# A convolution, attention and expert kernel: small operands moved to PSUM, row sums reordered, one norm partly on GpSimd

## The chip, the core and the metric

The kernel runs on one core of a Trainium2 chip, as one launch. The core has five engines, each with a queue of its own that is worked through in order: TensorE (PE in the profile, PEld where it loads weights), VectorE (DVE), ScalarE (ACT), GpSimd (POOL) and SyncE (SP, which here only issues transfers). The metric is the device time of the launch in microseconds. A ratio is the new time over the old one, so below 1 is faster.

## The reference, cut to what matters

Four images of 256 channels and 32 by 32 places (1024 tokens each) go through one layer:

```python
x = x + L0_conv_ref(_ln_c(x), ...)     # norm over channels, then the mixer below
t = _to_tokens(x)
t = t + L0_ffn_ref(_ln_t(t), ...)      # experts: 2 of 8 for each token

# the mixer, per image (names cut)
xn  = layernorm(xs); xc = xn in 4 groups of 64 channels
xm  = selective scan of each group (128 inner channels, 16 states) + skip * xc
R   = gated, depthwise and pointwise convolutions of xm
xm2 = convolutions of [xs, R]
x_local  = depthwise convolution of xm2
x_global = softmax attention of xm2, 8 heads of 32 channels
x_out = gelu(layernorm([x_local, x_global] @ fc.T))
out   = projection of layernorm(3x3 depthwise of ln_hw(x_out))

# the experts
top_w, top_i = top_k(xf @ Wg, 2); top_w = softmax(top_w)
out += w[:, e] * (gelu(xf @ W1[e] + b1[e]) @ W2[e] + b2[e])   # for each expert e
```

All data are float32. The softmax of a token's two gate values is computed as 1 / (1 + exp(m2 - m1)) and its complement.

## The kernel before, in words

**Order of the work.** The order on every engine is the order of the program text: a manual schedule fixes it. The program is made of Python generators that issue a few instructions and then `yield` a number of beats. A loop of beats (`beat`, `start`, `drain`) resumes each generator when its time has come, one after the other. So a generator that yields one beat more comes one beat later against all the others, on all engines, and the queues of the engines never change their order at run time.

**The scan.** Each image has eight parts (four groups, two halves of 512 tokens), and each part 16 steps; one step is one beat. A step works on a tile of 128 partitions (32 channels by 4 states) by 512 tokens: ACT makes the decay (L718, three steps ahead), DVE the inflow (`dBu`, L728) and the scan (L739), POOL multiplies by the output coefficients (L747), PE sums over the states (L757).

**Beside the scan.** While image b is scanned, other generators work on images before and after it. With part 3 of image b ends a first half; then come `attention(b - 1)` and the work joined to it (`joined`), `local(b - 1)`, the 3x3 convolution of image b - 2 (`around`) and the norm of the image b + 1 (`normalised`). Until 30 of attention's 32 steps are issued no step of the scan is issued; then `resume` starts part 4 and the rest runs beside it. For b = 1 this is the first attention, and `normalised(2)`, the third image's norm, starts in the same beat as it. The attention of the fourth image comes after all scans, between tiles of the experts.

**The norm of an image** (`normalised`, L524 on): after the loads, PE averages two chunks of 128 channels with a matrix of constants (`column_mean`, accumulating over the chunks), DVE subtracts the mean, POOL squares, PE averages the squares, ACT makes two roots (r1, r2). Then for each chunk POOL multiplies by r1 (L556), DVE by r2 (L558), SP stores the first product, POOL scales the second (L561), and for the third image `own_taps` adds one ACT and two DVE operations (L572, L579) and a store.

**Attention** (L1112 on): a step is one of two groups of four heads, one half of the queries and one block of 128 keys. PE makes the logits of the next step (`st`, L1126), ACT their exponentials (`e`, L1136), PE multiplies this step's by the values (`av<-e,v`, L1175). DVE adds the exponentials of an even and an odd block (L1183), and `sum_pair` (L1144) has PE sum the rows of the pair with a matrix of ones (`av<-e,every`, L1147). A pair is put on a list at the end of an odd step. It is summed at the head of the next odd step, or, in the last five steps, at the head of the next step whatever its parity, in both cases before the next logits are issued.

**Routing** (`dispatch`, L1797 on): with the norm's r (L1858) the gate values are scaled, `first_largest` finds the largest and the second largest of the eight (m_1, m_2) and their experts, one expert bit per token goes through two matmuls (`places`, L1886, L1887) to be counted, `ex` and `w_1` become the two weights (L1881, L1891, L1903 to L1911), and XR, the token's row with its number, weights and expert, is scattered by POOL to rows sorted by expert. `gp` and `cp` are banks in PSUM of which these steps cut pieces (`w1()`, `w3()`); m_1, m_2, r, mr, ex and w_1 are [128, 8, 1] tiles in SBUF. For the first two images (`beside`) the normalised rows are made by ACT from r and mr, for the others by DVE. Routing of image 0 runs beside the scan of image 2, that of image 1 beside the scan of image 3, the others between expert tiles.

**The tables.** `series` (L2133) and `table` (L2019) turn the counts into a list of tiles: which expert, and where its rows start. All of it is done by DVE on [128, 8] or [128, 8, 8] tiles. The table of the first series is made in the last part of the scan, at 1411 to 1420 us; those after it between expert tiles.

PSUM has eight tiles of one bank each, tag `ps`, from which each user takes the next free one. `a2` (16 tiles of 512) and `a4` (8 of 1024) are pools of SBUF tiles.

Of the kernel before, what the change touches and what calls it, by code (L numbers as in the profile page):

```python
# [78 lines left out]
def network(  # L79
# [71 lines left out]
    with tc.tile_pool(name="w_conv", bufs=1) as wp, tc.tile_pool(  # L151
# [251 lines left out]
        def a2(name, rows=P):  # L403
            return act2.tile([rows, HALF], F32, tag="a2", name=name)
# [118 lines left out]
        def normalised(b):  # L523


            place_xn(b)
            xn = XN[b]

            def part(c, h):
                return xn[:, c, ds(LEFT + h * HALF, HALF)]  # L530

            yield 4

            def centre(h, mean):
                for c in range(NC2):
                    nc.vector.tensor_tensor(part(c, h), part(c, h), mean, ALU.subtract)

            yield from in_turn(
                range(2), lambda h: column_mean(f"mean_{b}_{h}", [part(c, h) for c in range(NC2)]),
                centre,  # L540
            )
            r1, r2 = a4(f"r1_{b}"), a4(f"r2_{b}")
            for h in range(2):
                sq = [a2(f"sq_{b}_{h}_{c}") for c in range(NC2)]
                for c in range(NC2):
                    nc.gpsimd.tensor_tensor(sq[c], part(c, h), part(c, h), ALU.mult)
                yield 1
                var = column_mean(f"var_{b}_{h}", sq)
                yield 2
                root(r1[:, half(h)], var, eps6)  # L550
                yield 1
                root(r2[:, half(h)], var, eps11, scale=1.0 + 1e-5)
                yield 1
            for c in range(NC2):
                xl = a4(f"xl_{b}_{c}")
                nc.gpsimd.tensor_tensor(xl, xn[:, c, LEFT:], r1, ALU.mult)  # L556
                yield 2
                nc.vector.tensor_tensor(xn[:, c, LEFT:], xn[:, c, LEFT:], r2, ALU.mult)  # L558
                yield 1
                nc.sync.dma_start(XL[b][:, c, :], xl)  # L560
                nc.gpsimd.tensor_scalar(  # L561
                    xn[:, c, LEFT:], xn[:, c, LEFT:], col("norm_w", c), col("norm_b", c),
                    ALU.mult, ALU.add,
                )
                yield 1
                if b in XD and b < B - 1:
                    yield from own_taps(b, c, xl)
# [539 lines left out]
        def attention(b):  # L1107
# [32 lines left out]
            log_exp()  # L1140
            ahead = logits(*steps[0])
            pairs, accs, ending = [], [None, None], []

            def sum_pair():  # L1144
                kt, acc, es = pairs.pop()
# [18 lines left out]

            for at, (g, h, kt) in enumerate(steps):
                es = ahead
                if pairs and (kt % 2 or at > len(steps) - 6):
                    sum_pair()
                if at + 1 < len(steps):
                    ahead = logits(*steps[at + 1])  # L1170
                if kt == 0:

                    accs = [ps(f"av_{b}_{g}_{h}_{w}") for w in range(2)]
                for i in range(4):
                    nc.tensor.matmul(  # L1175
                        accs[0][ts(i, HD)], v8[:, kt, ts(4 * g + i, HD)], es[i],
                        start=(kt == 0), stop=(kt == NK - 1),
                    )
                if kt % 2 == 0:
                    first = es  # L1180
                else:
                    for i in range(4):
                        nc.vector.tensor_tensor(first[i], first[i], es[i], ALU.add)  # L1183
                    pairs.append((kt, accs[1], first))
                    if ending:
                        end_block(*ending.pop())
                if kt == NK - 1:
                    ending.append((g, h, *accs))
                if at == len(steps) - 3:
                    T["attended", b] = True  # L1190
                yield 1
# [204 lines left out]
        def tiles():  # L1396
# [28 lines left out]
            def table(n):  # L1425
                tables_of.add(n)
                s, i = order[n]
                if s < rest and i == 0:
                    tables[s] = experts.series(s, temp)

            def load(n):
                s, i = order[n]
# [206 lines left out]
class Experts:  # L1639
# [158 lines left out]
    def dispatch(self, b, X1, XR, root, log_exp, recent):  # L1798
# [67 lines left out]
        )  # L1866
        beside = b < self.B - 2
        if beside:
            mr = s1("mr")
            nc.vector.scalar_tensor_tensor(mr, mv[:, :, 0:1], -1.0, r, ALU.mult, ALU.mult)  # L1870
        m_1, oh1, at1 = self.first_largest(lg, "1", w1, eq)
        yield 1
        lg2 = lg
# [3 lines left out]

        oh = s3("oh")
        nc.vector.tensor_tensor(oh, oh1, oh2, ALU.add)
        ex, w_1 = s1("ex"), s1("w_1")  # L1880
        nc.vector.tensor_tensor(ex, m_2, m_1, ALU.subtract)  # L1881
        yield 4 if beside else 1
        cp = bank(f"places_{b}")
        flat = oh.rearrange("p t e -> p (t e)")
        W = NT * NE
        nc.tensor.matmul(cp[:, 0:W], self.before, flat, start=True, stop=True)  # L1886
        nc.tensor.matmul(cp[:, W : 2 * W], self.every, flat, start=True, stop=True)  # L1887

# [12 lines left out]
            if t % (4 if beside else 2) == 1:  # L1901
                yield 1
        nc.vector.tensor_scalar(w_1, ex, 1.0, None, ALU.add)  # L1903
        nc.vector.reciprocal(w_1, w_1)
        nc.gpsimd.iota(
            XR[:, :, C : C + 1], [[P, NT], [0, 1]], base=b * N, channel_multiplier=1,
            allow_small_or_imprecise_dtypes=True,
        )
        nc.vector.tensor_copy(XR[:, :, C + 1 : C + 2], w_1)
        nc.vector.tensor_tensor(ex, ex, w_1, ALU.mult)  # L1910
        nc.vector.tensor_tensor(XR[:, :, C + 2 : C + 3], ex, w_1, ALU.subtract)  # L1911
        nc.vector.tensor_scalar(XR[:, :, C + 3 : C + 4], at2, float(NE), None, ALU.add)
        yield 1

# [101 lines left out]
        nc.vector.tensor_reduce(ntile.rearrange("p a e -> p e a"), steps, AX.X, ALU.add)  # L2016
        return ntile

    def table(self, temp, keep, name, n, ntile, which, done=None, kinds=NE):  # L2019


        nc = self.nc
        ends = keep(f"ends_{name}", [P, 1, kinds])
        nc.vector.tensor_tensor_scan(
            ends[:, 0, :], self.every[:, 0:kinds], ntile[:, 0, :], 0.0, ALU.mult, ALU.add
        )
        starts = temp(f"starts_{name}", [P, 1, kinds])
        nc.vector.tensor_tensor(starts, ends, ntile, ALU.subtract)
        S = [P, n, kinds]
        past = temp(f"past_{name}", S)  # L2030
        nc.vector.tensor_tensor(past, which, ends.to_broadcast(S), ALU.is_ge)
        inside = temp(f"inside_{name}", S)
        nc.vector.tensor_tensor(inside, which, starts.to_broadcast(S), ALU.is_ge)
        nc.vector.tensor_tensor(inside, inside, past, ALU.subtract)
        expert = keep(f"expert_{name}", [P, n, 1])
        nc.vector.tensor_reduce(expert, past, AX.X, ALU.add)
        nc.vector.tensor_scalar(expert, expert, float(kinds - 1), None, ALU.min)
        if kinds > NE:
            second = temp(f"second_{name}", [P, n, 1])
            nc.vector.tensor_scalar(  # L2040
                second, expert, float(NE), float(-NE), ALU.is_ge, ALU.mult
            )
            nc.vector.tensor_tensor(expert, expert, second, ALU.add)

        nc.vector.tensor_tensor(which, which, starts.to_broadcast(S), ALU.subtract)
        if done is not None:
# [12 lines left out]
        table = self.m0.tile([P, 2, n], mybir.dt.int32, name=f"table_{name}")  # L2059
        nc.vector.tensor_copy(table[:, 0, :], expert.rearrange("p n a -> p (n a)"))  # L2060
        nc.vector.tensor_scalar(
            table[:, 1, :], first.rearrange("p n a -> p (n a)"), float(self.SPARE), None, ALU.add
        )
        return (expert, table), starts, ends
# [65 lines left out]
        nc.vector.tensor_copy(self.missed, self.sum_of(temp, "missed", missed))  # L2130
        return table

    def series(self, s, temp):  # L2133

        if s == self.WIDE:
            return self.wide_series(temp)
# [30 lines left out]
        if s:  # L2167
            nc.vector.tensor_tensor(ntile, ntile, self.done, ALU.subtract)
        table, starts, ends = self.table(
            temp, self.kept, s, n, ntile, which, self.done if s else None  # L2170
        )
        taken = temp(f"taken_{s}", [P, 1, NE])
        nc.vector.tensor_scalar(taken, starts, -1.0, float(n), ALU.mult, ALU.add)
# [346 lines left out]
```

## Time and profile before

| what | value |
|---|---|
| median of three runs | 2169.73 us (2165.35 to 2173.6) |
| profiled execution | 2167.03 us, its span 2165.3 us |
| PE busy | 1931.0 us, 89% of the span |
| DVE busy | 1540.5 us, 71% |
| ACT busy | 1212.3 us, 56% |
| POOL busy | 1043.4 us, 48% |
| mean granted clock of TensorE | 0.961 |

Shares over the whole span mix stages with different limits. The span goes, roughly, like this: preparation to 60 us; scans of the first images to 430; the first attention, 430 to 531; scans to 790; the second attention, 790 to 888; scans to 1190; the third attention, to 1290; the last scans to 1439; convolutions of the fourth image and expert tiles to 1592; the fourth attention to 1681; expert tiles, with the last image's end between them, to 2165. A row of the profile in order of time gives start and length in us, engine, line of the kernel, operation, what is written from what, shapes, and in brackets how long the engine had been idle and what released it. Buffer numbers are left out of the names, and rows that follow each other with the same line are merged (x4).

### The profile page before, as it was taken

How to read it: one execution, taken by the hardware profiler on the slowest of the kernel's cores; microseconds unless marked ns; L12 is line 12 of the kernel's file. 1: busy time of each engine (PE TensorE's matmuls, PEld its weight loads, DVE VectorE, ACT ScalarE, POOL GpSimd, SP SyncE). 2: the span in 40 equal slices, each digit the busy share in tenths (PEclk: the TensorE clock that was granted, in tenths of full speed). 3: DMA queues.
4: the chain of work that ended last, by engine and by line, in shares of the span. 5: the costliest groups of instructions: out<-in, count | busy, mean ns of one | idle time of the engine just before them, and what ended most of it. 6: DMA issues, size and time to landing. Idle time of an engine off the chain costs nothing. (4 is left out here: it accounts for less than half of the span.)

```text
span 2165.3 us, 28187 instructions
## 1 busy us (share of the span) xinstructions
PE 1931.0 (89%) x8690; PEld 867.6 (40%) x8690; DVE 1540.5 (71%) x2252; ACT 1212.3 (56%) x2272; POOL 1043.4 (48%) x931
## 2 busy tenths in 40 slices
PE   6778778999977999988779999669999989999996
PEld 2113112322211332223123223216652668888885
DVE  4989999957998989698899888987265354321121
ACT  4665657668777677776466876615268423222221
POOL 0887887812787850476877016662021012522131
PEclk8888999999999999998999999989999999999998
DMA  3555544401444431153634203444230165777764
GB/s 105 148 157 130 124 118 103 101 28 57 103 116 117 104 75 40 25 141 92 176 87 105 83 6 94 109 164 135 84 99 23 47 198 161 242 229 188 213 184 131
DMA packets 157087, 251.40 MB, mean 116 GB/s; under 512 B 34740, under 2 KB 101332, under 8 KB 156664
## 3 DMA queue, kind: packets, MB, share of 16 engines
q1 hardware_dynamic: 136560, 223.47, 37.3%
q0 software_dynamic: 12720, 17.32, 4.1%
q10 hardware_dynamic: 7640, 8.65, 1.2%
q8 instruction: 72, 1.18, 0.2%
q14 instruction: 95, 0.78, 0.1%
HBM read 137.22 MB, written 36.62 MB: 80 GB/s over the span
## 5 line engine op out<-in xcount | busy, mean ns | idle before, releaser
L747 POOL TENSOR_TENSOR dA<-hs,cs 128x512 f32<-128x512 f32 x512 | 681.1, 1339 | 376.9 <-DVE hs L739 249.8
L718 ACT ACTIVATE dA<-dts,A 128x512 f32<-128x512 f32 x512 | 359.0, 718 | 161.4 <-DMA dts<-dt 76.9
L757 PE MATMUL yp<-dA,quads 128*32 128x512 f32 x1024 | 286.3, 640 | 89.3 <-POOL dA L747 76.6
L2350 POOL DMA_INDIRECT Y<-ys,dest x68 | 109.6, 1612 | 424.3 <-DVE ys L2343 417.3
L1136 ACT ACTIVATE e<-st 128x512 f32<-128x512 f32 x512 | 263.7, 606 | 89.4 <-PE st L1126 89.2
L2337 ACT ACTIVATE hs<-h,b 128x256 f32<-128x256 f32 (+1 forms) x256 | 110.6, 478 | 343.6 <-PE h L2332 256.7
L728 DVE TENSOR_TENSOR dBu<-dts,bs 128x512 f32<-128x512 f32 x384 | 259.6, 677 | 46.0 <-PE bs L710 10.8
L739 DVE TENSOR_TENSOR_SCAN hs<-dA,last,dBu 128x512 f32<-128x512 f32 x192 | 243.6, 1269 | 3.0 <-issue 2.1
L2365 PE MATMUL y<-w,hs 128*128 128x256 f32 (+1 forms) x1088 | 242.4, 382 | 0.0
L2332 PE MATMUL h<-xT,w 128*128 128x256 f32 (+1 forms) x1024 | 239.7, 390 | 0.8 <-DVE xT L2295 0.8
L739 DVE TENSOR_TENSOR_SCAN hs<-dA,dBu 128x512 f32<-128x512 f32 x192 | 231.6, 1206 | 0.7 <-PE var L438 0.7
L1183 DVE TENSOR_TENSOR e<-e,e 128x512 f32<-128x512 f32 x256 | 168.2, 718 | 77.8 <-ACT e L1136 47.8
L2332 PEld LDWEIGHTS h<-xT,w 128*128 128x128 f32 x1024 | 195.2, 192 | 41.7 <-issue 8.0
L2365 PEld LDWEIGHTS y<-w,hs 128*128 128x128 f32 (+1 forms) x1088 | 197.3, 188 | 36.1 <-issue 9.0
L2295 DVE COPY xT<-xp 128x512 f32<-128x512 f32 (+1 forms) x36 | 23.3, 646 | 249.4 <-PE xp L2291 249.1
L710 PE MATMUL bs<-u,xpwT_s 128*32 128x512 f32 x1024 | 162.9, 669 | 40.3 <-DVE hs L739 17.3
L1126 PE MATMUL st<-qk 32*128 32x512 f32 x1024 | 174.0, 638 | 0.3
L757 PEld LDWEIGHTS yp<-dA,quads 128*32 128x32 f32 x1024 | 51.3, 114 | 303.4 <-POOL dA L747 198.7
L1175 PE MATMUL av<-e,v 128*32 128x512 f32 x1024 | 139.5, 604 | 0.0
L1953 POOL DMA_INDIRECT XS<-XR,to x64 | 65.4, 1022 | 92.0 <-ACT e L1136 53.9
L1126 PEld LDWEIGHTS st<-qk 32*128 32x128 f32 x1024 | 59.5, 183 | 115.3 <-issue 85.6
L1147 PE MATMUL av<-e,every 128*32 128x512 f32 x512 | 85.2, 596 | 2.7 <-DVE e L1183 2.6
(357 smaller groups left out, 2640.5 us busy)
## 6 DMA issues: line engine op xcount, KB each, us to landing
dts<-dt SPq DMA_DIRECT2D x512, 128.0 KB
w<-in_W_dram SPq DMA_DIRECT2D x124, 512.0 KB
cs<-cd SPq DMA_DIRECT2D x512, 64.0 KB
xs<-XS SPq DMA_DIRECT2D x32, 260.0 KB
xd<-xn SPq DMA_DIRECT2D x64, 128.0 KB
xn<-in_x_dram SPq DMA_DIRECT2D x8, 512.0 KB
XL<-xl SPq DMA_DIRECT2D x8, 512.0 KB
xl<-XL SPq DMA_DIRECT2D x4, 1024.0 KB
```

The source lines that it names most:

```text
L710: nc.tensor.matmul(bs[r], xpwT_s[:, n, s : s + 1].to_broadcast([P, 32]), T[b, n, "u"][:, half(h)], start=True, stop=True,)
L718: nc.scalar.activation(dA, T[b, n, h, "dts", g][:, 0, :], AF.Exp, scale=A[:, g, n, q : q + 1])
L728: nc.vector.tensor_tensor(dBu, T[b, n, h, "dts", g][:, 1, :], T[b, n, h, "bs", q], ALU.mult)
L739: nc.vector.tensor_tensor_scan(hs, T[b, n, h, "dA", i], dBu, 0.0 if h == 0 else last, ALU.mult, ALU.add)
L747: nc.gpsimd.tensor_tensor(dA, hs, T[b, n, h, "cs", q], ALU.mult)
L757: nc.tensor.matmul(T[b, n, h, "yp"][ts(g, 32)], quads, T[b, n, h, "dA", q * GD + g], start=False, stop=(q == GS - 1),)
L1126: nc.tensor.matmul(sts[i], k[r, ts(kt, P)], q[r, half(h)], start=True, stop=not shifted)
L1136: ins = nc.scalar.activation(es[i], sts[i], AF.Exp, scale=1.0 / HD**0.5)
L1175: nc.tensor.matmul(accs[0][ts(i, HD)], v8[:, kt, ts(4 * g + i, HD)], es[i], start=(kt == 0), stop=(kt == NK - 1),)
L1183: nc.vector.tensor_tensor(first[i], first[i], es[i], ALU.add)
L2332: nc.tensor.matmul(hp[:, i, :], w1(c, k0 + i), xT[:, c, :], start=(c == 0), stop=(c == NC2 - 1))
L2365: nc.tensor.matmul(yp[ts(k % parts, n), ts(t % 2, C)], hidden(k)[:, ds(t * P, n)], w2(k), start=(k < parts), stop=(k >= NHC - parts),)
```

## The change

Three parts of the program are edited.

1. Routing: the tiles ex and w_1 become pieces of the bank `places`, which is now claimed before the yield that stood between them and the matmuls. m_1 is copied to a piece of the gate's bank before it is subtracted; for the first two images ACT copies r to such a piece, and mr is made from the copy. The reciprocal is written to its column of XR at once, and the copy to that column (L1909) goes. The first table gets a bank of its own in PSUM: the counts are copied to it, and ends, starts and inside are pieces of it.
2. Attention: the rule that a pair is summed at the head of a step, before the logits, holds for the third image only. For the others a pair is summed in the next step, behind its product with the values.
3. Norm of the third image: POOL adds the two chunks, and later the two squares, so that `column_mean` gets one chunk instead of two. The sums and squares lie in halves of r1 and r2 and no longer in four `a2` tiles. The generator yields two beats more before the means and one more before each half's second step.

```diff
@@ normalised
+            r1, r2 = a4(f"r1_{b}"), a4(f"r2_{b}")
+            one_chunk = b == 2
+            if one_chunk:
+                for h in range(2):
+                    nc.gpsimd.tensor_tensor(r1[:, half(h)], part(0, h), part(1, h), ALU.add)
+                yield 2
             yield from in_turn(
-                range(2), lambda h: column_mean(f"mean_{b}_{h}", [part(c, h) for c in range(NC2)]),
+                range(2), lambda h: column_mean(
+                    f"mean_{b}_{h}",
+                    [r1[:, half(h)]] if one_chunk else [part(c, h) for c in range(NC2)],
+                ),
                 centre,
             )
-            r1, r2 = a4(f"r1_{b}"), a4(f"r2_{b}")
             for h in range(2):
-                sq = [a2(f"sq_{b}_{h}_{c}") for c in range(NC2)]
+                if one_chunk:
+                    sq = [v[:, half(h)] for v in (r1, r2)]
+                else:
+                    sq = [a2(f"sq_{b}_{h}_{c}") for c in range(NC2)]
                 for c in range(NC2):
                     nc.gpsimd.tensor_tensor(sq[c], part(c, h), part(c, h), ALU.mult)
+                if one_chunk:
+                    nc.gpsimd.tensor_tensor(sq[0], sq[0], sq.pop(), ALU.add)
+                    yield 1
                 yield 1
@@ attention
+            late = b == B - 2
...
-                if pairs and (kt % 2 or at > len(steps) - 6):
+                if late and pairs and (kt % 2 or at > len(steps) - 6):
                     sum_pair()
...
+                if pairs and not late:
+                    sum_pair()
                 if kt % 2 == 0:
                     first = es
@@ tiles
-                    tables[s] = experts.series(s, temp)
+                    tables[s] = experts.series(s, temp, None if s else ps("first_table"))
@@ dispatch
         if beside:
-            mr = s1("mr")
-            nc.vector.scalar_tensor_tensor(mr, mv[:, :, 0:1], -1.0, r, ALU.mult, ALU.mult)
+            mr, r_too = s1("mr"), w1()
+            nc.scalar.copy(r_too, r)
+            nc.vector.scalar_tensor_tensor(mr, mv[:, :, 0:1], -1.0, r_too, ALU.mult, ALU.mult)
...
-        ex, w_1 = s1("ex"), s1("w_1")
-        nc.vector.tensor_tensor(ex, m_2, m_1, ALU.subtract)
+        cp = bank(f"places_{b}")
+        W = NT * NE
+        ex, w_1 = (
+            cp[:, ds(7 * W + k * NT, NT)].rearrange("p (t a) -> p t a", a=1) for k in range(2)
+        )
+        first = w1()
+        nc.vector.tensor_copy(first, m_1)
+        nc.vector.tensor_tensor(ex, m_2, first, ALU.subtract)
         yield 4 if beside else 1
-        cp = bank(f"places_{b}")
         flat = oh.rearrange("p t e -> p (t e)")
-        W = NT * NE
...
         nc.vector.tensor_scalar(w_1, ex, 1.0, None, ALU.add)
-        nc.vector.reciprocal(w_1, w_1)
+        w_mine = XR[:, :, C + 1 : C + 2]
+        nc.vector.reciprocal(w_mine, w_1)
...
-        nc.vector.tensor_copy(XR[:, :, C + 1 : C + 2], w_1)
-        nc.vector.tensor_tensor(ex, ex, w_1, ALU.mult)
-        nc.vector.tensor_tensor(XR[:, :, C + 2 : C + 3], ex, w_1, ALU.subtract)
+        nc.vector.tensor_tensor(ex, ex, w_mine, ALU.mult)
+        nc.vector.tensor_tensor(XR[:, :, C + 2 : C + 3], ex, w_mine, ALU.subtract)
@@ table, with a bank
+            counts, ends, starts = (
+                bank[:, ts(k, kinds)].rearrange("p (a e) -> p a e", a=1) for k in range(3)
+            )
+            nc.vector.tensor_copy(counts, ntile)
         nc.vector.tensor_tensor_scan(
-            ends[:, 0, :], self.every[:, 0:kinds], ntile[:, 0, :], 0.0, ALU.mult, ALU.add
+            ends[:, 0, :], self.every[:, 0:kinds], counts[:, 0, :], 0.0, ALU.mult, ALU.add
         )
...
+            inside = bank[:, ds(3 * kinds, n * kinds)].rearrange("p (n e) -> p n e", e=kinds)
         nc.vector.tensor_tensor(inside, which, starts.to_broadcast(S), ALU.is_ge)
         nc.vector.tensor_tensor(inside, inside, past, ALU.subtract)
```

More of the change, by code (lines that the diff above doesn't have):

```diff
@@ L2017, in tiles_of, with table @@
         return ntile
-    def table(self, temp, keep, name, n, ntile, which, done=None, kinds=NE):
+    def table(self, temp, keep, name, n, ntile, which, done=None, kinds=NE, bank=None):
         nc = self.nc
-        ends = keep(f"ends_{name}", [P, 1, kinds])
+        if bank is None:
+            ends = keep(f"ends_{name}", [P, 1, kinds])
+            starts = temp(f"starts_{name}", [P, 1, kinds])
+            counts = ntile
+        else:
+            counts, ends, starts = (
+                bank[:, ts(k, kinds)].rearrange("p (a e) -> p a e", a=1) for k in range(3)
+            )
+            nc.vector.tensor_copy(counts, ntile)
         nc.vector.tensor_tensor_scan(
-            ends[:, 0, :], self.every[:, 0:kinds], ntile[:, 0, :], 0.0, ALU.mult, ALU.add
+            ends[:, 0, :], self.every[:, 0:kinds], counts[:, 0, :], 0.0, ALU.mult, ALU.add
         )
-        starts = temp(f"starts_{name}", [P, 1, kinds])
         nc.vector.tensor_tensor(starts, ends, ntile, ALU.subtract)
@@ L2031, in table @@
         nc.vector.tensor_tensor(past, which, ends.to_broadcast(S), ALU.is_ge)
-        inside = temp(f"inside_{name}", S)
+        if bank is None:
+            inside = temp(f"inside_{name}", S)
+        else:
+            inside = bank[:, ds(3 * kinds, n * kinds)].rearrange("p (n e) -> p n e", e=kinds)
         nc.vector.tensor_tensor(inside, which, starts.to_broadcast(S), ALU.is_ge)
@@ L2131, in wide_series, with series @@
         return table
-    def series(self, s, temp):
+    def series(self, s, temp, bank=None):
         if s == self.WIDE:
@@ L2169, in series @@
         table, starts, ends = self.table(
-            temp, self.kept, s, n, ntile, which, self.done if s else None
+            temp, self.kept, s, n, ntile, which, self.done if s else None, NE, bank
         )
```

## The prediction

> **What bounds the kernel now.** I read the page first (share of each engine), then the kernel cut into its stages, then the two engines' rows in order of time at each place that the diff touches. The chain that ended last is of no use here: its 18 pieces cover only the last 10 us (output rows and their transposes), which the change leaves alone.
>
> ```profile
> PE 1931.0 (89%) x8690; PEld 867.6 (40%) x8690; DVE 1540.5 (71%) x2252; ACT 1212.3 (56%) x2272; POOL 1043.4 (48%) x931
> 430.00:531.00 101.00, 100.60 (x652) 28.92 (x654) 65.53 (x85) 75.14 (x146) 19.33 (x14) 1.00 0.12 39
> 888.00:1190.00 302.00, 259.89 (x957) 84.36 (x950) 269.65 (x333) 198.37 (x362) 227.51 (x194) 0.94 0.43 112
> 1290.00:1439.00 149.00, 115.69 (x403) 35.03 (x400) 138.07 (x207) 81.54 (x155) 101.44 (x99) 0.90 0.39 107
> 1592.00:1681.00 89.00, 89.00 (x647) 25.66 (x646) 53.02 (x87) 69.97 (x138) 21.79 (x34) 1.00 0.15 44
> ```
>
> The last four are stages: start and end, length, then the busy time of PE, PEld, DVE, ACT and POOL. In the stages of attention (430 to 531 is the first, 1592 to 1681 the fourth) PE has no idle time. In those of the scan DVE is busy for 270 of 302 and 138 of 149 us. So a microsecond counts on PE in attention and on DVE in the scan.
>
> The second image's routing (L1903 to L1912), DVE then POOL:
>
> ```profile
> 1378.03 0.86 DVE L1903 TENSOR_SCALAR w<-ex 128x8 f32<-128x8 f32 x1
> 1378.93 0.20 DVE L1904 RECIPROCAL w<-w 128x8 f32<-128x8 f32 x1
> 1379.17 0.96 DVE L1909 COPY XR<-w 128x8 f32<-128x8 f32 x1
> 1380.04 1.30 DVE L1910 TENSOR_TENSOR ex<-ex,w 128x8 f32<-128x8 f32 x1
> 1381.37 0.18 DVE L1911 TENSOR_TENSOR XR<-ex,w 128x8 f32<-128x8 f32 x1
> ...
> 1377.58 1.28 POOL L672 TENSOR_TENSOR dt<-dt,u 128x512 f32<-128x512 f32 x1
> 1378.81 2.50 POOL L747 TENSOR_TENSOR dA<-hs,cs 128x512 f32<-128x512 f32 x2
> ```
>
> Eight numbers a partition take 0.86 to 1.30 us, and each slow row ends within 0.1 us of the end of a POOL product. With POOL quiet, the same rows of the third and fourth image take 0.16 to 0.17. The first table shows it more strongly:
>
> ```profile
> 1412.04 3.19 DVE L2024 TENSOR_TENSOR_SCAN ends<-every,ntile 128x8 f32<-128x8 f32 x1
> 1415.33 0.17 DVE L2028 TENSOR_TENSOR starts<-ends,ntile 128x8 f32<-128x8 f32 x1
> ...
> 1415.86 1.93 DVE L2034 TENSOR_TENSOR inside<-inside,past 128x64 f32<-128x64 f32 x1
> ```
>
> Its other two calls took 0.17 for the first of these rows and 0.23 for the last. Lastly, PE near the end of the first attention, and of the fourth:
>
> ```profile
> 522.73 1.07 PE L1175 MATMUL av<-e,v 128*32 128x512 f32 x8
> 523.62 1.66 PE L1147 MATMUL av<-e,every 128*32 128x512 f32 x6
> 525.68 1.05 PE L1147 MATMUL av<-e,every 128*32 128x512 f32 x2 [0.40 <-DVE e L1183]
> 526.65 1.14 PE L1126 MATMUL st<-qk 32*128 32x512 f32 x8
> ...
> 1673.17 1.58 PE L1147 MATMUL av<-e,every 128*32 128x512 f32 x8
> 1674.68 1.14 PE L1126 MATMUL st<-qk 32*128 32x512 f32 x8
> ...
> 1678.41 2.07 PE L1147 MATMUL av<-e,every 128*32 128x512 f32 x6
> ```
>
> Row sums (L1147) usually take 1.0 from start to start; here 3.03 (523.62 to 526.65) and 1.51, because DVE's pair additions are late, and the logits (L1126) stand behind them.
>
> **What the skill says.** The Trainium skill, "SBUF — State Buffer", section "Who interferes with whom": a DVE instruction with two SBUF inputs, or in a two-port mode, and a GpSimd instruction that reads SBUF exclude each other for a whole instruction; one with at most one SBUF input outside those modes doesn't. The rows above agree. "VectorE: DVE Perf Modes", section "Why PSUM operands drop a tier": an operand in PSUM rules the two-port mode out, so the moved copies and scalar operations should be free too; PSUM operands in the profile (gate, places) take 0.17 to 0.23 whatever POOL does. "PSUM — Partial Sum Buffer", section "PSUM bank collisions raise a hardware error": two engines may not use one bank at once, so they must be put in order. Hence ACT's exponential of ex will stand behind the two matmuls of places, now in its bank; before shows no such wait.
>
> **Part 1, small operands in PSUM.** The sum is made against the profiled execution, 2167.03 us, span 2165.3, 1.7 around it; that is 2.70 under the median of 2169.73.
> - First image: mr 1.08 to 0.15 (its other call) saves 0.93; w 0.92 to 0.17 saves 0.75; the copy into XR (L1909) goes, 0.87 from start to start; ex times w 1.33 to 0.20 saves 1.13. The added copy of m_1 costs 0.2 (L1928, a like copy, 0.16). Together -3.5. DVE has no gap there, so it counts.
> - Second image: mr was at 0.15 already; w -0.70, copy -0.87, product -1.13, added copy +0.2: -2.5.
> - ACT's added copy of r (0.2, by the row of ex, L1891) is issued one beat after r's root, and DVE's lg comes between: DVE doesn't wait for it. ACT's exponential waits for places: 1015.91 to about 1017.8 in the first image. Behind it stand the exponentials of the scan (L718), issued three steps ahead of use, 5.3 us at 1.77 a step: the 1.9 is covered. Without that cover it would cost 1.9.
> - First table: scan 3.29 to 0.4 with the added copy, inside 1.86 to 0.25: up to -4.5. But POOL's products at 1412.69 to 1417.70 still run, and three small operations stay SBUF to SBUF (the minimum, the scaling of which, the clamp): DVE meets the same products there, for about 1.3 us at most each. Bounds 0 and -4.5; I take -3.0, since the first of them would start near 1413.6, when 1.5 of POOL's pair is left. POOL, idle for 4.4 us after 1417.7 until DVE's next scan, starts earlier by as much, and so does its queue of products and row scatters, which ends this stage.
> - Third and fourth image: nothing to gain. In the fourth PE stood idle 2.15 us for oh, before places; the copy of m_1 and ex now come ahead of the matmul: +0.35.
> Sum: -8.65.
>
> **Part 2, sums behind the values.** In the loop's body the order on PE is mostly the same, since a sum at the end of an even step and one at the head of the next odd step are neighbours, other generators' matmuls apart. It differs in the last five steps. First attention: the sum at 523.62 goes behind the logits and values (2.0 us of work), by when the additions (ending 525.6) are done: -2.0. Fourth: the logits at 1674.68 come 1.5 earlier, so do their exponentials, and the last additions and sums, which end the stage at 1680.41; working the steps forward (logits 1673.1, values 1674.2, sums 1675.2, last values 1676.2, last sums 1677.2 to 1678.4) gives -2.0. Second: no stall to remove (its late sums lie earlier, where DVE is behind), 0. In the first two, step 30's logits lose a sum ahead of them but wait there for ACT anyway: 0, at worst +1. Sum: -4.0.
>
> **Part 3, norm of the third image, in the first attention.** PE loses four matmul groups: mean took 1.91 a half (449.42 to 451.33), var the same; one chunk in place of two saves 0.95 four times: -3.8. POOL gains four additions of 1.27 (by L668), 5.1 us, in a stage where it is busy 19 of 101 us: hidden, but for collisions with DVE's pair additions (two SBUF inputs): +0.5. The extra yields (2, 1, 1) shift the rest of the norm by four beats. Before, its DVE tail lies at the seam: xn times r2 at 521.16, the taps at 531.28 and 534.80. Four beats later all three lie among scan steps, 1.22 + 1.28 + 1.28 = 3.8, and meet POOL (the tap operations L462 average 1.76 in their mixed stages against 1.25 alone, so 0.5 each): 5.3. What they free: about 0.9 at 531.28, 1.26 at 534.80, and 0.4 of a wait for ACT, whose tap scaling (1.26 at 529.74) goes too: 2.6. Net +2.7. SP gets the same two stores, later, behind a scan step's loads; nobody waits for them in this stage. Sum: -0.6.
>
> **Total**: -8.65 - 4.0 - 0.6 = -13.2; from the median 2169.73, **2156.5 us**.
>
> **Rivals.**
> - *The gain shrinks on its way* (0.24). The table's DVE time only moves to the operations left in SBUF (-1 in place of -3), the norm's tail costs +5 (one L462 instruction took 5.43), and a third of the routing gain ends in waits for PE and ACT, as 20 of the 302 us to 1190 do. About -6: 2164.
> - *More than counted* (0.14). The table keeps 4.5, the norm's tail falls into waits for ACT and is free (-2.7), POOL too loses waits. About -18: 2152.
> - *Slower* (0.08). The bank of places is now claimed before the yield of four scan steps in the first two images, so eight steps run with one bank fewer, and DVE writes into it. If each step waits for a bank, the gain is gone from 1.7 us a step on; at 2.3 it ends near 2175. For it: DVE does wait for banks (1.49 behind ACT's qk copy). Against: right after, from 1013 to 1022, steps run without a gap while both banks are held.
> - That the change doesn't act (PSUM operands no faster) is excluded by the gate and places rows.
>
> **Numbers.** The forecast, -9 to -17 (2153 to 2161), has 0.54. A measurement of this kernel tells about 0.5% from no change, 10.8 us, so 2158.9; four fifths of the forecast's cases and the second rival lie below it: 0.57 and some of the first rival, **0.64** faster; **0.28** within; **0.08** slower. The range, 2146 to 2169, leaves out the slower end and the extremes of both rivals.
>
> **What would show it.** Right: L1903, L1910 and the first table's rows near 0.2; no L1909; L1147 at the end of the first and fourth attention near 1.0; half the mean and var matmuls in the first attention, scan resuming some 5 us earlier after the same start. Wrong: DVE or ACT gaps at ex or first_table, small operations as slow as before one row further down, taps of 2 us and more among the scan steps, or the gains of 1027 gone at the drain near 1190.

## The result

Over 22 runs each, the changed kernel takes 2162.68 us (median; 2155.04 to 2168.4) and the kernel before 2167.94 us (2163.98 to 2179.78). The ratio is 0.9972, 95% interval 0.9963 to 0.9981: 6.1 us less (4.1 to 8.0), a little under half of the 13.2 that the prediction gives. The range (2146 to 2169) holds it. The side doesn't: 0.64 stood on "faster by over 0.5%", and the gain is 0.28%. The profiled execution took 2160.25 us, its span 2158.5.

The profile after: the page's first line, then the same four stretches as before (start and end, length, busy PE, PEld, DVE, ACT and POOL, then TensorE's granted clock and the DMA columns).

```profile
PE 1921.5 (89%) x8682; PEld 866.5 (40%) x8682; DVE 1539.0 (71%) x2253; ACT 1212.5 (56%) x2274; POOL 1052.9 (49%) x935
430.00:531.00 101.00, 101.00 (x660) 29.93 (x658) 70.86 (x90) 78.37 (x152) 24.21 (x19) 1.00 0.15 44
888.00:1190.00 302.00, 256.23 (x986) 84.14 (x978) 269.13 (x336) 201.79 (x369) 231.25 (x197) 0.97 0.46 115
1290.00:1439.00 149.00, 114.53 (x404) 34.33 (x402) 132.97 (x209) 78.86 (x149) 106.60 (x106) 0.92 0.40 110
1592.00:1681.00 89.00, 89.00 (x624) 28.29 (x617) 48.16 (x77) 66.65 (x131) 16.00 (x28) 1.00 0.07 24
```

The windows are at fixed times while the work has moved, so they only show that nothing changed in kind: PE full in attention, DVE nearly full in the scan, though in the second routing's stage DVE is busy for 133 us in place of 138.

The edits themselves did what was foreseen. The second image's routing, DVE in order of time (start, duration):

```profile
1357.88 0.16 DVE L1888 SCALAR_TENSOR_TENSOR mr<-mv,gate 128x8 f32<-128x8 f32 x1 [0.31 <-ACT gate L1887]
...
1373.89 0.15 DVE L1925 TENSOR_SCALAR places<-places 128x8 f32<-128x8 f32 x1
1374.08 0.21 DVE L1927 RECIPROCAL XR<-places 128x8 f32<-128x8 f32 x1
1374.32 0.17 DVE L1932 TENSOR_TENSOR places<-places,XR 128x8 f32<-128x8 f32 x1
1374.53 0.17 DVE L1933 TENSOR_TENSOR XR<-places,XR 128x8 f32<-128x8 f32 x1
...
1373.44 1.29 POOL L686 TENSOR_TENSOR dt<-dt,u 128x512 f32<-128x512 f32 x1
```

The rows that took 0.86 and 1.30 are at 0.15 and 0.17 although a product on POOL runs at the same time (the last row), and the copy that took 0.96 is gone. But mr, first in this list, waits 0.31 for ACT's copy of r. Now the first table, DVE and then POOL:

```profile
1405.42 0.18 DVE L2054 TENSOR_TENSOR_SCAN first_table<-every,first_table 128x8 f32<-128x8 f32 x1
...
1406.43 0.23 DVE L2066 TENSOR_TENSOR first_table<-first_table,past 128x64 f32<-128x64 f32 x1
...
1406.81 1.62 DVE L2069 TENSOR_SCALAR expert<-expert 128x8 f32<-128x8 f32 x1
...
1409.55 1.38 DVE L2092 CAST table<-expert 128x8 int32<-128x8 f32 x1
...
1407.10 1.26 POOL L761 TENSOR_TENSOR dA<-hs,cs 128x512 f32<-128x512 f32 x1
...
1409.61 1.28 POOL L761 TENSOR_TENSOR dA<-hs,cs 128x512 f32<-128x512 f32 x1
```

The two DVE rows of 1.62 and 1.38 in the kernel before:

```profile
1417.96 0.17 DVE L2037 TENSOR_SCALAR expert<-expert 128x8 f32<-128x8 f32 x1
...
1419.24 0.16 DVE L2060 CAST table<-expert 128x8 int32<-128x8 f32 x1
```

The scan falls from 3.19 to 0.18 and `inside` from 1.93 to 0.23. Two rows that read SBUF, which took 0.17 and 0.16 before, now take 1.62 and 1.38, and each ends within 0.1 us of the end of a POOL product: the wait for POOL's products moved on to them. PE at the end of the first attention, then of the fourth:

```profile
525.37 1.04 PE L1162 MATMUL av<-e,every 128*32 128x512 f32 x8
...
1668.58 2.14 PE L1162 MATMUL av<-e,every 128*32 128x512 f32 x8
```

In the first the sums run without a stall. In the fourth the last ones still take 2.14 for eight.

**How the traces were compared.** The order on each engine hardly changes, so the k-th scan instruction and the k-th matmul of each kind can be paired, and the start after minus the start before gives an offset. An edit's worth at its place is the step of the offset there. In this pair of traces: first attention and the seam behind it, where the scan resumes (2.68 to -0.04), -2.7; first image's routing -2.8; second image's -2.05; the first table -1.7; fourth attention -1.3; fourth image's places +0.37. But the offset also jumps where no edited instruction has run: +3.2 near 400 us, -2.8 near 975 us; and in the last stage it rises by 2.8 (-9.76 at 1714 us, -6.9 near 2050), of which the places explain 0.37. So the two spans don't show which part was worth what, and the experiments ask two things: are these jumps chance, and how much of each local step arrives at the end.

### The profile page after: what moved, and what is told of

It is laid out like the page before. It is cut to its first block, busy times and chain, and to the rows that moved or that the text cites. A ratio compares the mean times of both kernels' runs of the same rounds, so it can differ in the third digit from the quotient of the medians.

```text
span 2158.5 us, 28179 instructions
## 1 busy us (share of the span) xinstructions
PE 1921.5 (89%) x8682; PEld 866.5 (40%) x8682; DVE 1539.0 (71%) x2253; ACT 1212.5 (56%) x2274; POOL 1052.9 (49%) x935
## 3 DMA queue, kind: packets, MB, share of 16 engines
q10 hardware_dynamic: 7640, 8.65, 1.3%
q8 instruction: 72, 1.18, 0.2%
## 5 line engine op out<-in xcount | busy, mean ns | idle before, releaser
L724 PE MATMUL bs<-u,xpwT_s 128*32 128x512 f32 x1024 | 157.4, 651 | 39.7 <-DVE hs L753 15.0
L742 DVE TENSOR_TENSOR bs<-dts,bs 128x512 f32<-128x512 f32 x128 | 86.2, 673 | 0.9 <-DMA dts<-dt 0.9
```

The source lines that it names most:

```text
L724: nc.tensor.matmul(bs[r], xpwT_s[:, n, s : s + 1].to_broadcast([P, 32]), T[b, n, "u"][:, half(h)], start=True, stop=True,)
L742: nc.vector.tensor_tensor(dBu, T[b, n, h, "dts", g][:, 1, :], T[b, n, h, "bs", q], ALU.mult)
```

## Experiments

Several kernels below take one part of the change alone. "Offset" is against the first trace of the kernel before, and a "step" is the offset behind an edited place minus the offset ahead of it. Each ratio is to runs of the kernel before taken together with the kernel's own. 95% intervals are in brackets.

### The kernel before, once more

No edit.

> The kernel before, unchanged, for a second trace of it. If the offsets of about 3 us between traces, at stages where no edited instruction has run (by 405 us, by 777 us and by 990 us), are chance of the single execution, this trace has them against the first one too: TensorE rows that take 1.06 in place of 0.59 for some 6 us at a place where DVE waits for bs, then a wait of 2.8 on DVE. If they belong to the edited kernels, this trace stands within 0.5 us of the first up to the end.

Measured: one run, 2166.63 us, span 2164.9. Its offset against the first trace is +0.35 at the start, -1.05 at 390, +2.13 at 420, then -1.5 at 991; in the last stage it rises by 1.5. So jumps of this size come without any edit. What they are made of is seen in one stretch, the first trace and then the second; the column before the last two is the granted clock:

```profile
380.00:400.00 20.00, 18.44 (x64) 6.38 (x64) 19.83 (x24) 12.07 (x27) 17.96 (x14) 1.00 0.39 92
```

```profile
380.00:400.00 20.00, 19.49 (x59) 6.12 (x60) 17.21 (x21) 11.05 (x24) 16.25 (x13) 0.83 0.34 78
```

and DVE in the second trace:

```profile
397.04 0.70 DVE L728 TENSOR_TENSOR dBu<-dts,bs 128x512 f32<-128x512 f32 x1 [2.76 <-PE bs L710]
```

From 381 to 388 us the second trace has TensorE groups of 1.93 and 2.08 where the first has 1.06 and 1.12. Then `bs` is late and DVE loses 2.76. By the clock that the traces record, each has 26 to 35 such stretches, all at half clock, most of them 3.41 or 6.83 us long.

The Trainium skill ("TensorE: Matmul & The Clock Gate", section "What's actually happening") says that the clock is set by how busy TensorE was in a window of about 3.4 us that runs free of the kernel's start, so that where it falls varies from run to run. The traces agree: in all 14 the stretches begin on a grid of 3.41 us, and where the grid lies against the kernel's start differs between traces. Just before 740 us PE is idle for 2.10 us in the first trace of before as in that of the second part alone. Cut along each trace's own grid (length, busy PE, granted clock, DMA columns), the second part alone and then before:

```profile
737.30:740.71 3.41, 1.31 (x3) 1.00 0.01 2
740.71:744.13 3.42, 3.42 (x11) 0.50 0.01 2
744.13:747.54 3.41, 3.41 (x10) 0.50 0.26 77
```

```profile
735.70:739.11 3.41, 1.70 (x4) 1.00 0.04 11
739.11:742.52 3.41, 3.02 (x12) 1.00 0.02 5
```

In the first the idle time lies whole in one window, and the next two windows run at half clock. In the second the grid splits it, and none does. A `bs` that DVE waits for follows. In the seven traces with two slow windows from about 740 us on, DVE loses 3.2 us, in the two with one 1.6, in the other five nothing. So these jumps come in units of 1.6 us, and an edit that shifts the work by a microsecond may make or remove one (not tested).

The clock of each run tells the same. Over the 259 runs for which it was compared, with a mean of its own for every kernel, 0.001 more granted clock goes with 0.70 us less (0.58 to 0.82). About a third of the variance within a kernel goes with it; for the second and the third part alone, 14 runs each, no such relation is seen. The first part alone ran at a mean clock of 0.9607 where before beside it had 0.9584, so by this slope 1.6 of its gain could be the clock's.

### Each part alone, and the change without the third

The first part alone is the diff's lines in `tiles`, `dispatch`, `table` and `series`; the others are:

```diff
 # the second part alone, in attention
+            late = b == B - 2
-                if pairs and (kt % 2 or at > len(steps) - 6):
+                if late and pairs and (kt % 2 or at > len(steps) - 6):
...
+                if pairs and not late:
+                    sum_pair()
 # the third part alone: the diff's lines in normalised
 # the change without the third part
-            one_chunk = b == 2
+            one_chunk = False
```

> Only the small operands in PSUM, on the kernel before. By the forecast's sum: -8.65 us, ratio 0.9960; each image's routing and the first table gain -3.5, -2.5, -3.0, the fourth image loses 0.35 at its bank of places. By the shrunken sum that the two traces suggest: -2.6, -2.4 and -1.7, +0.4, so -6.3, ratio 0.9971, which is all that the whole change showed. By the rival that the bank of places costs: DVE or ACT waits at ex, and the ratio is 1.000 or above.

Measured: 2160.93 us, ratio 0.9976 [0.9963, 0.9988]: -5.2 us. Steps at the edited places: -2.8, -2.05, -1.7 and +0.37, together -6.2. The shrunken sum holds (the forecast's 0.9960 lies outside the interval), and the rival in which the bank of places costs is out.

> Only the sums behind the values, in three attentions. By the forecast: -2.0 in the first attention, 0 in the second, -2.0 in the fourth: -4.0, ratio 0.9981. By the traces: -2.0 and -1.3, so 0.9985. If the last stage gives the gain back (about 3 us were lost in it between the two traces), 1.0 us or less is left: ratio 0.9995 or above, with the fourth attention's gain there and gone 100 us later.

Measured: 2167.50 us, ratio 1.0003 [0.9994, 1.0012]: no gain. Steps: -1.75 in the first attention and -1.3 in the fourth, as in the change, and in the second +1.2 at its end, +1.05 over the whole of it. Even with that loss, -2.0 should have arrived, which is outside the interval. The last stage takes nothing back: the offset is 1.12 at 1714 us and 1.18 at the end.

> Only the third image's norm on GpSimd. By the forecast: TensorE -3.8 in the first attention, then +3.2 at the seam behind it: the scan starts some 3.8 earlier and stands 0.6 earlier eight steps on; ratio 0.9997. By the rival in which the shifted tail costs more (5 us): +1.2 after the seam, ratio 1.0006. If the tail is hidden: -3.3, ratio 0.9985.

Measured: 2167.88 us, ratio 0.9994 [0.9981, 1.0007]. Steps: -3.7 within the first attention (to 512 us), +1.4 from there on, -2.35 in all. The interval is too wide to tell this from the forecast's -0.6. PE at the end of the first attention:

```profile
524.81 1.88 PE L1161 MATMUL av<-e,every 128*32 128x512 f32 x8
526.62 1.14 PE L1140 MATMUL st<-qk 32*128 32x512 f32 x8
```

The sums take 1.81 from start to start where before has 3.03: DVE's product of xn, which stood ahead of the pair additions (521.16 in before), now comes later. So the third part takes away some of the stall that the second part is aimed at, and their steps there don't add: -2.35 and -1.75 alone, -2.7 together.

> The change without its third part. By the forecast -12.65, ratio 0.9942, 0.6 us behind the whole change. By the traces' shrunken sum -9.6, ratio 0.9956, if the loss in the last stage is chance; if the third part's shifted tail is what ate the gain, this kernel is 2 to 3 us faster than the whole change's 0.9972: 0.9960; if the gain is lost elsewhere, it is the same as the whole change.

Measured: 2163.26 us, ratio 0.9984 [0.9976, 0.9992]: -3.5 us. That is, if anything, behind the whole change, so the third part's shifted steps did not eat the gain. The local steps add to -8.2 here, and 4.7 of it doesn't arrive. It points at the second part again, since this kernel is no faster than the first part alone.

### The table's remaining operands in PSUM as well

On the changed kernel (of the table only the first one):

```diff
-        nc.vector.tensor_reduce(expert, past, AX.X, ALU.add)
-        nc.vector.tensor_scalar(expert, expert, float(kinds - 1), None, ALU.min)
+        nc.vector.tensor_reduce(whole, past, AX.X, ALU.add)      # whole, moved: slices of bank
+        nc.vector.tensor_scalar(whole, whole, float(kinds - 1), None, ALU.min)
+        nc.vector.tensor_copy(expert, whole)
-        nc.vector.tensor_tensor(which, which, starts.to_broadcast(S), ALU.subtract)
+        nc.vector.tensor_tensor(moved, which, starts.to_broadcast(S), ALU.subtract)
...
-        nc.vector.tensor_copy(table[:, 0, :], expert...)
+        nc.vector.tensor_copy(table[:, 0, :], whole...)
```

`first` and `taken` are slices of the bank too.

> The whole change, with the small operands of the first table that were left in SBUF (the minimum, the scaling of which, the cast's source, the clamp) in PSUM too, and one copy more. If the table's wait only moved on to these: the minimum 1.62 and the cast 1.38 fall to 0.2 each, +0.2 for the copy, -2.4 us from the table's end on; ratio to before 0.9961 where the change had 0.9972. If the wait moves on again to the three rows with two SBUF operands, or DVE waits for GpSimd's product of the next step anyway: no gain, 0.9972.

Measured: 2160.56 us, ratio 0.9959 [0.9944, 0.9974], where the change alone has 0.9972 [0.9963, 0.9981]. The intervals overlap, but the place is clear: the step at the table is -3.65 in place of -1.7. The two rows in a later kernel with the same table:

```profile
1403.42 0.17 DVE L2073 TENSOR_SCALAR first_table<-first_table 128x8 f32<-128x8 f32 x1
...
1405.13 0.17 DVE L2101 CAST table<-first_table 128x8 int32<-128x8 f32 x1
```

1.62 and 1.38 have become 0.17 each, and no row behind them became slow. (The minimum runs beside a POOL product here; the cast does not, so its row alone would not show that its operand's place did it.)

### The third part without its added yields

```diff
             if one_chunk:
                 ... the two sums on GpSimd
-                yield 2
...
                     nc.gpsimd.tensor_tensor(sq[0], sq[0], sq.pop(), ALU.add)
-                    yield 1
```

> The third part alone on the kernel before, without its three added yields, so that the norm's later steps stay in the scheduling beats where they were. By the forecast's terms: TensorE -3.8, collisions on GpSimd +0.5, and no shifted tail (+2.7 gone): -3.3 after the seam, ratio 0.9985. If TensorE then waits for GpSimd's sums at mean and var (they are issued one beat after their inputs, 1.3 us each): one to two waits of 1 to 2 us in the first attention, and -1 or nothing is left: 0.9995 to 1.0000. Where the tail's cost was not what took the gain, the offset behind the seam is that of the third part with its yields, -2.4.

Measured: 2168.78 us, ratio 0.9995 [0.9983, 1.0007]. Steps: -2.5 within the attention, and 0 behind it. With the yields it was -3.7 and +1.4. So the yields keep TensorE from waiting for GpSimd (1.2 us) and cost 1.4 in the shifted steps: a wash, and not what limits this part.

### Sums in front in the second attention too, alone and in a combined kernel

Alone, on the kernel before:

```diff
 # the second part alone, but
-            late = b == B - 2
+            late = b in (1, B - 2)
```

> The second part alone on the kernel before, with the sums left in front of the logits in the second attention as well as in the third, so behind the values in the first and fourth only. By the offsets at the edited places: -1.75 and -1.3, and the second attention's +1.2 gone: -3.05 us, ratio 0.9986. If these local gains don't reach the end, as the second part alone (1.0003) said: 0.9995 or above.

This kernel ran last, after the combined ones below. Measured: 2166.46 us, ratio 0.9988 [0.9978, 0.9999]: -2.6 us, where the second part as in the change had 1.0003 [0.9994, 1.0012]. The local gains of the first and fourth attention can be seen to arrive, and the kernels differ only in the second attention; but the two intervals still touch. The traces are clearer: in all four kernels with the sums behind the values in the second attention its step is +1.05, and in the nine others it is 0.

PE at the end of the second attention, first in the second part alone (sums behind the values):

```profile
890.72 1.04 PE L710 MATMUL bs<-u,xpwT_s 128*32 128x512 f32 x8
...
892.75 1.13 PE L1126 MATMUL st<-qk 32*128 32x512 f32 x4
894.62 1.46 PE L1126 MATMUL st<-qk 32*128 32x512 f32 x4 [0.74 <-DVE hs L739]
...
898.69 1.96 PE L438 MATMUL var<-sq,ones_mean 128*128 128x512 f32 x4 [0.76 <-ACT e L1136]
...
903.69 2.25 PE L1148 MATMUL av<-e,every 128*32 128x512 f32 x6 [0.36 <-DVE e L1186]
905.87 1.55 PE L629 MATMUL zp<-xn,inzT_s 64*128 64x512 f32 x3
```

then in the combined kernel below (sums in front):

```profile
886.23 1.04 PE L724 MATMUL bs<-u,xpwT_s 128*32 128x512 f32 x8
...
888.25 1.06 PE L1162 MATMUL av<-e,every 128*32 128x512 f32 x8
889.25 2.93 PE L1140 MATMUL st<-qk 32*128 32x512 f32 x8
892.11 1.07 PE L1190 MATMUL av<-e,v 128*32 128x512 f32 x8
...
896.76 3.30 PE L1162 MATMUL av<-e,every 128*32 128x512 f32 x8
899.99 1.98 PE L643 MATMUL zp<-xn,inzT_s 64*128 64x512 f32 x4
```

From `bs` to `zp` both hold the same matmuls in another order: 15.15 us with the sums behind, 13.76 with them in front. The logits are slow in both: in front they take 2.93 where 1.14 is usual, but a sum has filled 1 us ahead of them, and nothing between them and the last sums waits. Behind, PE reaches them sooner, half of them wait 0.74 for a scan step on DVE to end, then `var` waits 0.76 for ACT's exponentials, and the last sums 0.36 for the pair additions.

The end of the first attention, where the scan also starts beside the last steps, gives back as much. PE in the second part alone:

```profile
534.89 1.78 PE L1126 MATMUL st<-qk 32*128 32x512 f32 x4 [0.42 <-DVE hs L739]
...
540.49 1.05 PE L1148 MATMUL av<-e,every 128*32 128x512 f32 x2 [0.24 <-DVE e L1186]
542.16 2.25 PE L1148 MATMUL av<-e,every 128*32 128x512 f32 x6 [0.63 <-DVE e L1186]
```

The offset is 2.92 ahead of this attention, -0.04 where the scan resumes and 1.16 from 544 us on. So the stall taken away is worth 3.0, and the step of -1.75 is what is left after a loss of 1.2. No run leaves only the end of the first attention in front.

The combined kernel is the changed kernel with the table's remaining operands, without the third part, with `late` as above, and with ex and w in the gate's bank:

```diff
-        cp = bank(f"places_{b}")
-        ex, w_1 = (cp[:, ds(7 * W + k * NT, NT)]... for k in range(2))
-        first = w1()
+        pair = w3().rearrange("p t e -> p (t e)")
+        ex, w_1, first = (pair[:, ts(k, NT)]... for k in range(3))
...
         yield 4 if beside else 1
+        cp = bank(f"places_{b}")
```

> Without the third part; the small operands of the table wholly in PSUM, ex and w in the bank of the gate's logits in place of that of places (so the matmuls of places wait for oh alone), and the sums in front of the logits in the second attention too. From the traces of the parts: first part -6.2, the table's rest -2.4, ex's bank -0.4 (TensorE's wait in the fourth image 2.5 back to 2.15), the sums -1.75 in the first and -1.3 in the fourth attention, and the +1.2 of the second attention gone: -12, ratio 0.9944. If what the second part gains in place is lost again, as its 1.0003 says: -9, 0.9958.

Measured: 2156.95 us, ratio 0.9946 [0.9928, 0.9964]: -11.7 us, by an expected -12. TensorE's wait ahead of places in the fourth image is 2.15 again, for oh, where the change has 2.52, for ex. The second attention's step is 0.

> The combined kernel once more, beside the two below: ratio to before 0.9946 again, between 0.9935 and 0.9960, with the same offsets at the edited places (-2.8 and -2.1 at the two routings, -3.6 at the table, -1.75 and -1.3 in the first and fourth attention) and other offsets of about 3 us elsewhere.

Measured: 2158.49 us, ratio 0.9934 [0.9920, 0.9948], just below the range expected; the steps at the edited places are the same ones.

> The combined kernel with the sums in front of the logits in all four attentions, as before: the second part taken away alone. If its local gains of 1.75 and 1.3 reach the end: 3 us slower than the combined kernel, 0.9960 where that has 0.9946. If they are lost again further on, as the second part alone showed: the same as the combined kernel within 0.0007.

Measured: 2161.86 us, ratio 0.9947 [0.9931, 0.9962]: 2.8 us slower than the combined kernel that ran beside it (0.9934), by an expected 3. With five or six runs each the intervals overlap, so this supports the reading that these gains arrive and doesn't prove it alone. All three kernels of this group are 2 to 6 us faster against before than their local steps add to, so its ratios are better compared with each other than with the earlier ones.

> The combined kernel with the third part as in the change. By the offsets between traces at the seam behind the first attention (both parts together -2.7, the second alone -1.75): 1.0 us faster than the combined kernel, 0.9941 where that has 0.9946. If the norm's later steps cost more than they free: DVE's offset behind the seam is no better than the combined kernel's, and the ratio is 0.9946 or above.

Measured: 2153.70 us, ratio 0.9915 [0.9900, 0.9929]. The step behind the first attention is -2.7 in place of -1.75, so the third part adds its 1.0; the ratio moved by 4 us, three more than the place shows, on four runs. This kernel beats the change: its interval lies wholly under that of the change (0.9963 to 0.9981). With that of the combined kernel beside it (0.9920 to 0.9948) it overlaps.

### All runs together

Every run of these kernels and of before (303), fitted by least squares with one mean for before per batch of runs and one value per part (95% intervals; it takes the parts to add up):

| part | forecast | step at its place | fitted to the times |
|---|---|---|---|
| small operands, as in the change | -8.65 | -6.2 | -5.2 ± 1.3 |
| sums, first and fourth attention | -4.0 | -3.05 | -2.9 ± 1.7 |
| sums, second attention | 0, at worst +1 | +1.05 | +3.5 ± 1.9 |
| third image's norm | -0.6 | -2.4 alone, -1.0 beside the sums | -1.2 ± 1.1 |
| the four, as in the change | -13.2 | -9.2 | -5.8 (measured -6.1) |
| table's rest, ex in the gate's bank | not in the change | -2.3 | -4.1 ± 2.0 |

With the granted clock of each run as one more term (281 runs have it on record), small operands come out at -4.0 ± 1.2 and the second attention at +3.2 ± 1.6; the others move by 0.2 or less. Of the 7.1 us between forecast and result the edited places show 4: the first table 1.3, the two routings 1.15, the second attention 1.05, the first and fourth attention 0.95, less 0.4 that the norm gained beyond its forecast. The other 3 are found at no edited place.

## Why the prediction was right or wrong

- **Routing: mechanism right, 1.2 us too much.** Forecast -3.5 and -2.5, measured -2.8 and -2.05. The rows became as short as said (-2.75 and -2.70 at w, the copy and the product). The step that failed is "DVE doesn't wait for it" of ACT's copy of r: DVE waits 0.31 in both images. In the first, mr with this wait gains 0.51 in place of 0.93; in the second, where mr was fast already, the step there costs 0.35. With the added copy of m_1 the step is +0.30, where 0.2 was said. The wait foreseen for ACT's exponential of ex behind the matmuls of places came (2.81 in the first image) and, as said, costs DVE nothing.
- **First table: -1.7 in place of -3.0**, inside the stated bounds of 0 and -4.5. The three operations named as left in SBUF were bounded at 1.3 "at most each", and one such wait, 1.5, was taken off. Two came, together 2.7: the minimum took 1.62 in place of 0.17, and one that was not named, the cast, 1.38 in place of 0.16. With all of them moved the step is -3.65.
- **Fourth image: +0.35, measured +0.37**, with PE waiting for ex as foreseen; ex in another bank takes it away.
- **Sums, first attention: -2.0, measured -1.75, near by luck.** The stall was worth 3.0, and 1.2 was lost at the attention's end. Fourth: -2.0, measured -1.3; the last eight sums were put at 1.2 us and took 2.14.
- **Sums, second attention: the step that failed.** The prediction saw that "step 30's logits lose a sum ahead of them" and took it that they "wait there for ACT anyway: 0, at worst +1". The move costs 1.2 at the end of the first and of the second attention: the logits wait for the scan on DVE, and matmuls and sums behind them wait too. In the second no stall stands against it, and +1.05 is left, about the worst case given. The times show +3.5 ± 1.9; what the part beyond the local step comes from is open. With 0 there, the fitted sum would be -9.3.
- **Norm: -0.6, fitted -1.2 ± 1.1.** TensorE's -3.8 is confirmed (-3.7). The shifted tail and the collisions were put at +3.2; what follows the -3.7 costs 1.4 with this part alone and 2.7 beside the moved sums, whose stall it shares. The scan resumed 5.75 us earlier after the same start, for the 5 said. From there on the offset rises by 2.1 with this part alone, by 1.2 with the sums alone and by 3.0 with both (-3.06 to -0.04).
- **The rivals.** "The gain shrinks on its way" gave 2164, nearest to the result, but its causes are too small: the table's moved wait took 1.3, the two routings fell short by 1.15, and the norm's tail cost no more than was counted. What made up most of the difference isn't in it. The slower rival is excluded: eight steps with one bank fewer, and no new wait for a bank.
- **The side.** The bound of 0.5% is 10.8 us. A sum of -13.2 from about a dozen terms of 1 to 4 us stood 2.4 beyond it, so one or two terms mis-sized were enough to cross it. 0.64 was too much for that distance.

## What to carry to other kernels

A wait like that of DVE for POOL's products goes to the next instruction of the chain that meets them (of 4.5 us taken away at the first table, 2.7 came back): move a whole chain of small operands, or count the rest of the chain as cost. When matmuls change places in a queue, price the new order at every place where it acts, also where the old order had no stall, because the work moved away may have been what covered a wait: one edit here gained 3.0 and lost 1.2 within 20 us. Two parts that remove the same stall don't add. Effects of 1 to 3 us in a kernel of 2 ms can be read by pairing instructions between traces, but only from the step at the edit's own place, with a second trace of the unchanged kernel to show what jumps by itself.

## What was not expected of the hardware

TensorE runs at half clock in stretches of 3.41 or 6.83 us for the most part (groups of 1.06 take 1.93), 26 to 35 in each trace, on a grid whose place varies between executions of one kernel. In eleven traces the same idle time of 2.10 us stands before 740 us. As the grid cut it, it was followed by two slow windows (seven traces), one (two) or none (two), and 3.2, 1.6 or 0 us were lost at the `bs` behind it. Within a kernel, 0.001 of mean clock goes with 0.70 us of time.
